# A three-layer graph kernel on TensorE: norm stages tied behind evacuations, a row addition moved to the layer before, the output stores moved off Pool, and node sums kept in PSUM

## The chip, the cores and the metric

One Trainium2 chip, one of its cores. The metric is the time of one launch on the device, in microseconds (us). Before the change it was 1362.92 us (median of 3 runs, 1360.43 to 1364.69). Besides times there is one profile of every kernel, of one of its runs; "the trace" is what that profile recorded.

Names: PE is the tensor engine, DVE the vector engine, ACT the scalar engine, Pool the GpSimd engine, SP the sync engine, which here only issues DMAs.

## The reference, cut to what matters

```python
# x: (8, 2048, 64), adj: (2048, 2048), fp32; every layer: x = x + f(relu(layernorm(x)))
# layer 0: Chebyshev terms of adj, combined with weights of each node
out = einsum('bnki,nkio->bno', [h, A h, 2 A A h - h], einsum('nd,dkio->nkio', emb, weight)) + emb @ bias
# layer 1: three steps v = W2 relu(W1 [v, A v] + b1) + b2
# layer 2: agg = A h; (agg * c) @ w_nl folded, + b_nl; then @ w_out.T + b_out
# layer 3: attention masked by adj > 0.5; elu(att @ h)
```

The kernel tests at run time that no element of adj is above 0.5 (a general path stands by). Then every row's attention is uniform, and layer 3 adds one row for each batch, elu(mean over the nodes of h). This is why the kernel needs "the sums of h": h is the normalised, rectified x after layer 2, and its sum over 2048 nodes decides one row y that is added to all of x at the end.

## The kernel before

The eight batches are worked in four pairs p; the nodes in four blocks nb of 512. The heavy work is `product`: 32 matmuls of 128x512 that multiply one block of adj with all of h, ended by one DVE instruction (the evacuation) that takes the PSUM bank to SBUF. The `fill` functions are called after some of the 16 steps of a product, to emit other work there. A tile scheduler orders each engine's queue by its own estimate; an engine runs its queue in that order.

```python
pending = []
def norm_stages(xt, name, done, out_):       # layernorm + relu, in three stages
    z = block("z", f"z_{name}", 3)           # three buffers with the tag "z"
    ...                                      # DVE mean, z = x - mean; ACT square
    yield
    ...                                      # DVE var                        (L159, L160)
    nc.gpsimd.tensor_tensor(rstd, var, mhalf, op=ALU.pow)                   # (L162)
    yield
    nc.vector.scalar_tensor_tensor(h, g, 0.0, rstd, op0=max, op1=mult)      # (L165), cut
    done(h)
    yield

def go_on():                                 # one more stage of every pending norm
    for e in list(pending):
        next(e[0]); e[1] -= 1
        if e[1] == 0: pending.remove(e)

def product(hl, nb, name, out, crow, fill={}):
    ps = bank("mm", f"bv_{name}")
    for m in range(NCH):                     # 16 steps
        ...                                  # two matmuls bv (L202)
        if m in fill: fill[m]()
    nc.vector.tensor_tensor(out, ps, crow, op=ALU.mult)      # evacuation: g or e (L208)

def keep(p, nb, acc, name):                  # end of layers 0 and 1
    nc.gpsimd.dma_start(xs[p][:, part(nb), :], acc)
    norm_relu(acc, name, lambda z: nc.gpsimd.dma_start(hs[p][:, part(nb), :], z))

def node_weights(p, nb, terms):              # layer 0
    for t in range(4):
        for dg in range(D // DG):
            ...                              # PE: y (L458); DVE: 8 x L467, accumulates into acc, odd
        go_on()
    ...

def layer2(n, p):
    zsum = lastp.tile([P, 4, 2 * C], F32, name="zsum")
    def finish(nb):
        fill_x(acc, 2, p, nb)                                        # load of x
        nc.gpsimd.tensor_tensor(acc, acc, rows4(rbo), op=ALU.add)    # row addition (L664)
        pn = back_to_nodes(e[nb], wos, f"2_{p}_{nb}")                # PE: bn (L543)
        nc.vector.tensor_tensor(acc, pn, acc, op=ALU.add)            # (L666)
        norm_relu(acc, ..., add, zsum if nb == 0 else None)          # add: zsum += h (L670)
    for nb in range(NB):
        fill = {1: go_on, 4: lambda: behind(nb), 11: go_on}          # behind: finish(nb - 1)
        e.append(product(..., fill=fill))
    finish(3)
    prepare(n + 1, 3)
    all_done()
    pS = ...                                 # PE: sum of zsum over the nodes, 4 matmuls (L692)
    ...                                      # y = elu(pS / N); acc += y (L701); 8 stores on Pool (L703)
```

## Time and profile before

| | before |
|---|---|
| time, median | 1362.92 us |
| span of the profiled run, clock | 1363.3 us, 0.967 |
| PE busy | 1266.1 us of 1363.3 |
| layer 2, first to last product | 168.6 us |
| after the last product | 26.0 us |

PE is busy for 93% of the span. The page's lines, the waits and the stretches that show it are in the prediction. Two single places more: the first product of layer 2, and the end of a pair. Timeline of the kernel before (start us, duration us, engine, line, operation, out<-in, shapes, count; in brackets how long the engine idled, and for whom):

```profile
1177.99 0.69 DVE L165 SCALAR_TENSOR_TENSOR z<-z,rstd 128x512 f32<-128x512 f32 x1 [2.14 <-POOL rstd L162]
1178.60 0.68 DVE L208 TENSOR_TENSOR e<-bv,crow 128x512 f32<-128x512 f32 x1
...
1179.33 1.16 PE L543 MATMUL bn<-wl,e 128*128 128x128 f32 x8 [2.43 <-DVE e L208]
...
1219.05 2.08 PE L692 MATMUL pS<-zsum,ones 128*128 128x128 f32 x8 [2.67 <-DVE zsum L670]
```

The first bn waits 2.43 us for e, and e waits in DVE's queue behind a norm stage of layer 1 that is waiting for Pool's rstd. At a pair's end PE idles 2.67 us until the sums of h are in zsum, and the matmuls after that run slow (2.08 us for what takes 1.05 to 1.16 elsewhere).

### The profile page before, as it was taken

To read this page: it belongs to the slowest core of one execution; us is meant where nothing else is said; L and a number is where in the kernel's file an instruction comes from. 1 tells how busy PE (TensorE), PEld (TensorE's weight loads), DVE (VectorE), ACT (ScalarE), POOL (GpSimd) and SP (SyncE) were. 2 spreads that over 40 slices of the span, in tenths; PEclk is the share of its full clock that TensorE was granted. 3 is DMA by queue.
4 is the path that set the end of the run, shared out by engine and by line. 5 is a ranking of instruction groups with operands and counts; after the bars stand their busy time and mean duration, and the time that the engine had idled before them with its cause. 6 is when DMAs were issued, how large, how long until landed. Compare 5 with 4: busy or idle time off the path is not lost. (4 is left out here: it accounts for less than half of the span.)

```text
span 1363.3 us, 16001 instructions
## 1 busy us (share of the span) xinstructions
PE 1266.1 (93%) x5904; PEld 898.6 (66%) x5904; DVE 803.7 (59%) x1949; ACT 191.2 (14%) x325; POOL 227.8 (17%) x230
## 2 busy tenths in 40 slices
PE   6899999999999999999978999999999999888883
PEld 4678555555575555755556788788788877666762
DVE  4753677767775777267778744335324424665664
ACT  4542001000010000000011111112112112111100
POOL 1310011110020001010010013004002201333443
PEclk7799999999999999999988999999999999999896
DMA  6755223212122112111067623113103212323231
GB/s 193 217 193 119 82 81 96 78 62 66 59 82 61 55 50 68 53 35 62 32 214 232 191 77 101 31 33 136 34 30 103 76 31 77 123 90 97 78 86 34
DMA packets 95595, 123.45 MB, mean 91 GB/s; under 512 B 50804, under 2 KB 52852, under 8 KB 95508
## 3 DMA queue, kind: packets, MB, share of 16 engines
q1 hardware_dynamic: 76180, 92.69, 22.5%
q0 software_dynamic: 8784, 27.41, 5.8%
q10 hardware_dynamic: 10544, 2.23, 0.8%
q8 instruction: 49, 0.80, 0.2%
q14 instruction: 38, 0.31, 0.1%
HBM read 94.90 MB, written 27.40 MB: 90 GB/s over the span
## 5 line engine op out<-in xcount | busy, mean ns | idle before, releaser
L202 PE MATMUL bv<-BT,H 128*128 128x512 f32 x1024 | 423.2, 413 | 0.0
L202 PE MATMUL bv<-BT,L 128*128 128x512 f32 x1024 | 404.6, 395 | 0.4 <-DVE L L194 0.4
L202 PEld LDWEIGHTS bv<-BT,L 128*128 128x128 f32 x1024 | 194.9, 190 | 48.5 <-issue 9.3
L202 PEld LDWEIGHTS bv<-BT,H 128*128 128x128 f32 x1024 | 194.8, 190 | 47.8 <-issue 9.3
L467 DVE SCALAR_TENSOR_TENSOR acc<-y,emb,acc 128x128 f32<-128x128 f32 x512 | 176.4, 345 | 63.4 <-PE y L458 63.2
L467 DVE SCALAR_TENSOR_TENSOR odd<-y,emb,odd 128x128 f32<-128x128 f32 x448 | 153.6, 343 | 0.0
L458 PE MATMUL y<-wt,t0T 64*128 64x512 f32 x512 | 139.9, 609 | 10.7 <-DVE odd L467 10.7
L440 POOL DMA_DIRECT2D xs<-acc x32 | 17.6, 551 | 742.1 <-DVE acc L471 382.6
L162 POOL TENSOR_TENSOR rstd<-var,mhalf 128x8 f32<-128x8 f32 x64 | 106.8, 1669 | 187.3 <-DVE var L160 179.0
L208 DVE TENSOR_TENSOR g<-bv,crow 128x512 f32<-128x512 f32 x48 | 33.1, 690 | 136.6 <-PE bv L202 136.6
L165 DVE SCALAR_TENSOR_TENSOR z<-z,rstd 128x512 f32<-128x512 f32 x60 | 51.1, 852 | 102.0 <-POOL rstd L162 102.0
L156 ACT ACTIVATE sq<-z 128x512 f32<-128x512 f32 x64 | 40.5, 633 | 454.1 <-DVE z L152 444.2
L458 PEld LDWEIGHTS y<-wt,t0T 64*128 64x128 f32 x512 | 44.1, 186 | 74.9 <-issue 69.7
L543 PE MATMUL bn<-wl,g 128*128 128x128 f32 x384 | 52.2, 280 | 8.2 <-ACT g L634 8.2
L543 PEld LDWEIGHTS bn<-wl,g 128*128 128x128 f32 x384 | 49.9, 194 | 14.1 <-ACT g L634 11.4
L580 DVE SCALAR_TENSOR_TENSOR junk<-st,cols 128x512 uint8<-128x512 f32 x64 | 48.5, 758 | 17.1 <-DMA st<-in_adj_dram 15.9
L159 DVE TENSOR_REDUCE var<-sq 128x8 f32<-128x512 f32 x64 | 43.7, 683 | 24.3 <-ACT sq L156 24.2
L215 PE MATMUL pt_adj<-ident,st 128*128 128x128 f32 x256 | 43.1, 314 | 14.1 <-DMA st<-in_adj_dram 10.4
L286 DVE TENSOR_REDUCE cols<-st 128x1 f32<-128x1024 f32 x32 | 38.9, 1216 | 27.1 <-DMA st<-in_adj_dram 27.0
L215 PEld LDWEIGHTS pt_adj<-ident,st 128*128 128x128 f32 x256 | 34.1, 161 | 24.3 <-issue 10.5
L150 DVE TENSOR_REDUCE mean<-acc 128x8 f32<-128x512 f32 x64 | 43.4, 684 | 3.9 <-DMA acc<-in_x_dram 2.3
L152 DVE TENSOR_TENSOR z<-acc,mean 128x512 f32<-128x512 f32 x64 | 43.9, 693 | 1.8 <-DVE var L160 0.3
(178 smaller groups left out, 1758.8 us busy)
## 6 DMA issues: line engine op xcount, KB each, us to landing
st<-in_adj_dram SPq DMA_DIRECT2D x32, 512.0 KB, 4.7
crow<-crowD SPq DMA_DIRECT2D x64, 256.0 KB, 3.2
st<-in_adj_dram SPq DMA_DIRECT2D x64, 256.0 KB, 3.5
hs<-z POOLq DMA_DIRECT2D x48, 256.0 KB, 3.0
hb<-hs SPq DMA_DIRECT2D x40, 256.0 KB, 3.2
xs<-acc POOLq DMA_DIRECT2D x32, 256.0 KB, 2.5
acc<-xs SPq DMA_DIRECT2D x32, 256.0 KB, 2.9
acc<-in_x_dram SPq DMA_DIRECT2D x48, 128.0 KB, 2.8
```

The costliest lines, as they stand in the source:

```text
L150: nc.vector.tensor_reduce(mean, groups(xt), axis=AX.X, op=ALU.add)
L152: nc.vector.tensor_tensor(g, groups(xt), mean[:, :, None].to_broadcast([P, 8, C]), op=ALU.subtract)
L156: nc.scalar.activation(sq, z, AF.Square)
L159: nc.vector.tensor_reduce(var, groups(sq), axis=AX.X, op=ALU.add)
L162: nc.gpsimd.tensor_tensor(rstd, var, mhalf, op=ALU.pow)
L165: nc.vector.scalar_tensor_tensor(groups(h), g, 0.0, rstd[:, :, None].to_broadcast([P, 8, C]), op0=ALU.max, op1=ALU.mult)
L202: nc.tensor.matmul(ps, hl[m // 4][i][:, m % 4, :], BT[:, nb, m, :], start=(m == 0 and i == 0), stop=(m == NCH - 1 and i == 1),)
L215: nc.tensor.transpose(pt[:, t, :], src(t), ident)
L458: nc.tensor.matmul(y[:, bb, :], terms[k][hs_, ts], wt[hs_, k, dg * 512:(dg + 1) * 512], start=(k == 0), stop=(k == K - 1),)
L467: nc.vector.scalar_tensor_tensor(xj, yd, ec, old, op0=ALU.mult, op1=ALU.add)
L543: nc.tensor.matmul(ps[:, t, :], fT[:, t * P:(t + 1) * P], wmat, start=True, stop=True)
L580: nc.vector.scalar_tensor_tensor(junk, tested[k], cols[:, i, :], tested[k], op0=ALU.not_equal, op1=ALU.logical_and, accum_out=bad[:, i, q: ...
```

## The change

Its intent: take from DVE's queue what stands ahead of an evacuation, take from Pool what slows DVE, take the additions of h from DVE, and issue the stores on queues with hardware descriptors. The core of the diff:

```diff
+    ahead = []
     def go_on():
-        for e in list(pending):
-            ...
+        with tc.issue_after(ahead.pop().ins) if ahead else nullcontext():
+            for e in list(pending):
+                ...
+        ahead.clear()
# product:
-        nc.vector.tensor_tensor(out, ps, crow, op=ALU.mult)
+        ahead.append(nc.vector.tensor_tensor(out, ps, crow, op=ALU.mult))
# node_weights: the last L467 of a tile goes into ahead before go_on
+            ahead.append(last)
             go_on()
# keep: the row of layer 2's bias is added at the end of layer 1, after the norm has read acc
-    def keep(p, nb, acc, name):
-        nc.gpsimd.dma_start(xs[p][:, part(nb), :], acc)
+    def keep(p, nb, acc, name, more=None):
         norm_relu(acc, name, lambda z: nc.gpsimd.dma_start(hs[p][:, part(nb), :], z))
+        if more is not None:
+            nc.gpsimd.tensor_tensor(acc, acc, more, op=ALU.add)
+        nc.gpsimd.dma_start(xs[p][:, part(nb), :], acc)
# layer2:
-            nc.gpsimd.tensor_tensor(acc, acc, rows4(rbo), op=ALU.add)
-            norm_relu(acc, f"3_{p}_{nb}", add, zsum if nb == 0 else None)
+            norm_relu(acc, f"3_{p}_{nb}", lambda h: z.update({nb: h}))
+        def sums(nb):
+            for t in range(4):
+                nc.tensor.matmul(pS[:, :2 * C], ones, z[nb][:, t, :],
+                    start=(nb == 0 and t == 0), stop=(nb == NB - 1 and t == 3))
         def behind(nb):
+            go_on()
-            fill = {1: go_on, 4: lambda: behind(nb), 11: go_on}
+            fill = {5: lambda: behind(nb), 12: go_on}
+            if nb > 1:
+                fill[15] = lambda: sums(nb - 2)
+        go_on()
         finish(3)
+        sums(2)
         prepare(n + 1, 3)
         all_done()
-        pS = bank("tr", f"pS_{p}")
-        for t in range(4):
-            nc.tensor.matmul(pS[:, :2 * C], ones, zsum[:, t, :], start=(t == 0), stop=(t == 3))
+        sums(3)
# the stores:
-                nc.gpsimd.dma_start(
+                (nc.scalar if p == NP - 1 and nb % 2 else nc.sync).dma_start(
```

`issue_after` orders the queue of the engine: what is emitted inside comes after the named instruction. If `ahead` is empty, nothing is ordered. The lines shift: L162 becomes L163, L165 L166, L194 L197, L202 L205, L208 L211, L458 L463, L467 L472, L543 L549, L692 L676, L703 L713; the row addition L664 becomes L445.

## The prediction

> **What bounds the kernel now.** I read the page's busy times and slices first, then the waits of TensorE, then the busy times by stretch, then single stalls in the timeline. The first three lines are from the page: busy time, then forty slices of about 34 us.
>
> ```profile
> PE 1266.1 (93%) x5904; PEld 898.6 (66%) x5904; DVE 803.7 (59%) x1949; ACT 191.2 (14%) x325; POOL 227.8 (17%) x230
> PE   6899999999999999999978999999999999888883
> PEclk7799999999999999999988999999999999999896
> ```
>
> TensorE is the bound: only 97 us of the 1363 are idle. The slices say where: the start, the change from layer 0 to layer 1 (about 690 us), and the last six, which are layer 2. Layer 1 (800 to 1168 us) is full. So Pool at 17% and DVE at 59% can matter only through waits that they give TensorE. Those are (us in total, times, longest):
>
> ```profile
> PE bn L543 <- DVE e L208: 21.5, 10, 3.1
> PE pS L692 <- DVE zsum L670: 14.2, 4, 7.4
> PE y L458 <- DVE odd L467: 10.7, 7, 2.4
> ```
>
> The first two are layer 2, the third is layer 0; all three are touched by the change. Two stretches, layer 2 up to the end of its last product, and the tail (us; PE, PEld, DVE, ACT, POOL busy with counts; granted clock; DMA share; GB/s):
>
> ```profile
> 1168.70:1337.70 169.00, 143.11 (x651) 117.23 (x650) 106.88 (x172) 17.82 (x30) 68.05 (x60) 0.94 0.29 86
> 1337.70:1363.30 25.60, 3.24 (x16) 2.75 (x16) 10.11 (x18) 0.94 (x2) 8.12 (x10) 0.57 0.18 44
> ```
>
> TensorE idles 25.9 of 169 us, at a clock of 0.94, and then the kernel runs 25.6 us without a product. One stall of layer 2 in order of time (start, duration):
>
> ```profile
> 1239.39 1.26 POOL L664 TENSOR_TENSOR acc<-acc,wl 128x512 f32<-128x512 f32 x1
> 1239.45 1.74 DVE L165 SCALAR_TENSOR_TENSOR z<-z,rstd 128x512 f32<-128x512 f32 x1 [1.83 <-POOL rstd L162]
> 1241.23 0.69 DVE L670 TENSOR_TENSOR zsum<-zsum,z 128x512 f32<-128x512 f32 x1
> 1241.84 0.68 DVE L208 TENSOR_TENSOR e<-bv,crow 128x512 f32<-128x512 f32 x1
> 1242.57 2.08 PE L543 MATMUL bn<-wl,e 128*128 128x128 f32 x8 [3.11 <-DVE e L208]
> ```
>
> The product had long ended. DVE could not evacuate it (e), because the last norm stage (L165) stood ahead of e in its queue, waited 1.83 us for Pool's rstd, ran 1.74 us instead of the 0.69 us it takes elsewhere, and was followed by the zsum addition. After 3.11 us of idleness the eight bn matmuls take 2.08 us; after shorter gaps they take 1.16. The same pattern in layer 0:
>
> ```profile
> 242.62 0.69 DVE L165 SCALAR_TENSOR_TENSOR z<-z,rstd 128x512 f32<-128x512 f32 x1 [1.85 <-POOL rstd L162]
> 243.23 0.35 DVE L467 SCALAR_TENSOR_TENSOR acc<-y,emb,acc 128x128 f32<-128x128 f32 x1
> 245.53 1.97 PE L458 MATMUL y<-wt,t0T 64*128 64x512 f32 x4 [2.10 <-DVE odd L467]
> ```
>
> **What the Trainium skill says.** (1) "SBUF — State Buffer", Who interferes with whom: a DVE instruction with two SBUF inputs contends with a GpSimd instruction that reads SBUF, and one blocks fully. The trace agrees: of the 18 L165 in layer 2, 13 start within 0.1 us after an L664 addition on Pool and take 1.74 to 1.78 us; the other five take 0.69. (2) "TensorE: Matmul & The Clock Gate", Architectural detail: ScalarE's and VectorE's queues are strict FIFO. The stall above is that. (3) Same page, What's actually happening: about 3.4 us of idleness halve the clock and about as much work restores it. Here gaps of 2.7 to 3.1 us are already followed by slices at 0.53 to 0.85, so this bites somewhat earlier, which a free-running window allows. (4) "DMA: Bandwidth & Descriptors", SWDGE vs HWDGE vs iDMA: Pool's DMAs have descriptors made by software, those of SP and ACT by hardware, with faster setup. Here one store takes 0.75 us of Pool (L703), one load 0.32 to 0.43 us of SP.
>
> **The change, part by part.** *Ties.* Every go_on now queues its DVE norm stages behind the last evacuation (or, in layer 0, behind the last L467 of a tile). In layer 2 the stages move to products' steps 5 and 12. So e runs as soon as its product ends, 0.1 + 0.68 us. bn stands 12 matmuls (12 x 0.226, start to start, = 2.7 us) into the next product: no wait. Of 21.5 us of bn waits, 2.45 belong to the last bn (tail); of the other 19.0 I keep 1 us at the first product, where stages left from layer 1 still precede e.
>
> *Row addition.* 16 Pool additions of 1.3 us move from layer 2 to the end of layer 1, where TensorE has no idle time to lose and Pool is nearly empty. L165 loses its 1.06 us extra 13 times, all off the bound once e is tied ahead; it shortens the final chain of each pair.
>
> *Sums.* The 12 zsum additions (0.69 us of DVE) go; instead TensorE does 16 blocks of 4 matmuls where it did 4. A block's 8 records cost 0.92 us, as bn does from its start to the next product's matmul (1179.33 to 1180.25). Within the stretch 14 blocks replace 3: +11 x 0.95 = +10.4 us on the bound, a real price. Blocks two products behind are ready without a wait. At the end of a pair, the chain bn, acc, mean, z, square, var, rstd, z is 7.6 us without the Pool wait, the slow L165 and the addition (10.7 before); TensorE reached the old pS 7.7 us after bn. So of 6.8 us of waits in the first three pairs about 2.5 remain.
>
> *Clock.* In layer 2 the product matmuls average 404 ns against 389 in undisturbed stretches: 505 x 15 ns = 7.6 us, with slow bn and pS about 10. With gaps below 1 us nearly all of it returns.
>
> Layer 2 up to its last product: 143.1 busy - 10 cold + 10.4 sums + 3.5 idle left + 1.5 of transitions = 148.5 us, for 169: **-20.5 us**.
>
> *Tail.* Four lines of the timeline:
>
> ```profile
> 1341.35 0.69 DVE L666 TENSOR_TENSOR acc<-bn,acc 128x512 f32<-128x512 f32 x1 [1.31 <-issue]
> 1348.64 2.08 PE L692 MATMUL pS<-zsum,ones 128*128 128x128 f32 x8 [7.39 <-DVE zsum L670]
> 1352.02 2.50 DVE L701 TENSOR_TENSOR acc<-acc,y 128x512 f32<-128x512 f32 x4
> 1353.01 6.01 POOL L703 DMA_DIRECT2D out_dram<-acc  x8 [5.87 <-DVE acc L701]
> ```
>
> e comes 1.6 us sooner, the zsum addition (0.7) is off the chain. Pool's eight stores end at 1359.0, 4.5 us after the additions; on two hardware queues the last pair is issued about 0.8 us after its addition: some 3.3 us saved with landing. Together **-5.5 us**.
>
> *Layer 0.* Four gaps of pair 0 (1.8, 1.8, 2.1, 2.4) come from L165 ahead of L467; tied, the two stages run behind the 16 L467 of the first tile. They then cost 1.4 us of DVE there, against its slack of 2 x 0.5 us (8 x 0.258 for a y that TensorE makes in 2.57), leaving about 0.4 each: 6.5 saved. Two of these gaps are followed by a clock of 0.96 over 40 us, 1.6 us each: 3 saved. A wait of 2.0 at 413 us (transposes for an evacuation behind L165) goes too. The other three y waits (2.6 us together) come from a halved operand (L194), not from a stage, and stay. With a margin for new small waits: **-10 us**.
>
> Sum: 1362.9 - 20.5 - 5.5 - 10 = 1327, which I round to **1328 us**.
>
> **Rivals.** (a) *The sums eat the gain.* The price of 10 us is on the bound; if blocks also wait for z, or break the weight-load overlap and cost 1.3 us each, layer 2 gains only 13 and the total is near 1336. For it: an unwarmed pS takes 2.08. Against: warmed, 8 records take 0.92 to 1.2. (b) *The wait moves.* Stages behind e make z late, so each pair's end, or the next pair's first e behind the y chain on DVE, stalls instead: 3 us a pair returned, near 1338. Against: 7.6 against 7.7 us, though that margin is thin. (c) *SP blocks.* The stores wait on SP for the additions, with loads of crow and acc behind them in the queue; 2 us a pair would give 1334. Against: eight issues of 0.35 us are 2.8 us, and the next loads are needed several us later. (d) *Layer 0 gives nothing*, because the stages then hold L467 elsewhere: 1338. (e) Better: the clock stays up everywhere and no gap is left, 1320.
>
> **Range and chances.** Each rival costs 6 to 10 us and two together are plausible; all of them are not. I take 1316 to 1342. The 2% line is 1335.7, some 8 us above the estimate: faster by over 2% 0.72, within 2% 0.27, slower 0.01.
>
> **What would show it.** Right: the bn wait for e below 4 us in total, L165 in layer 2 at 0.69, DVE running e before L165, pS records fourfold (128) at about 0.12 us each, clock above 0.98 in layer 2, y waits near 4 us, no store on Pool's list, and a tail of about 20 us. Wrong: bn or pS still waiting 3 us at pair ends, a clock still below 0.96, y waits of 8 us or more, or layer 1 with new idle time from the moved additions.

## The result, and the profile after

The changed kernel took **1340.24 us** (median of 4 runs, 1335.47 to 1340.92) beside 1361.68 us of the kernel before on the same chip; the ratio is 0.9836, 95% interval 0.9802 to 0.9870. A ratio is the mean time of one kernel's fast runs over that of the other's of the same rounds, so not quite the ratio of the medians quoted. It is faster by 1.6%, "the same" at a line of 2%. The prediction's range held it; its point was 12 us too low, and its likeliest class was wrong.

The page after: busy times, and the slices (tenths busy, tenths of the clock):

```profile
PE 1266.3 (95%) x6000; PEld 904.0 (68%) x6000; DVE 777.1 (58%) x1937; ACT 192.0 (14%) x325; POOL 202.9 (15%) x198
...
PE   6899999999999999999979999999999999989995
```

PE has 96 matmuls more (6000 for 5904) and the same busy time, and the span is 24 us shorter. The waits of PE after (us in total, times, longest):

```profile
PE pS L676 <- DVE z L166: 10.6, 7, 5.3
...
PE y L463 <- DVE odd L472: 8.6, 8, 2.7
...
PE bn L549 <- DVE e L211: 6.6, 3, 5.2
```

bn's wait for e fell from 21.5 to 6.6, but of that one single wait is 5.2. The wait for the sums comes seven times now, not four. The two stretches after, layer 2 to the end of its last product and the tail (columns as in the prediction):

```profile
1162.10:1317.70 155.60, 143.69 (x731) 121.12 (x730) 87.44 (x165) 17.69 (x30) 35.39 (x27) 0.98 0.33 97
1317.70:1339.10 21.40, 4.67 (x28) 3.91 (x26) 8.01 (x16) 0.94 (x2) 2.40 (x2) 0.67 0.23 54
```

PE idles 11.9 us in layer 2 for 25.9 before. To see where the 24 us came from, the span is cut at single matmuls that both kernels have: first matmuls of products, for layer 1 the first transpose of its operand, for layer 2 the matmul after layer 1's last bn, and for the tail the start of the last product matmul. A second profile of the changed kernel (e11 below), from a later chip, shows what repeats:

| stretch, us | before | after | after, again | predicted change |
|---|---|---|---|---|
| prologue | 136.7 | 138.6 | 136.2 | 0 |
| layer 0, pairs 0 and 1 | 247.3 | 238.2 | 238.5 | |
| layer 0, first terms of pair 2 | 32.8 | 30.6 | 30.6 | |
| layer 0, rest to the third part of pair 3 | 213.7 | 218.0 | 216.2 | |
| layer 0, these three | 493.8 | 486.8 | 485.3 | -10 |
| from there to layer 1 | 64.2 | 64.2 | 64.3 | 0 |
| layer 1 | 473.9 | 471.6 | 472.5 | 0 |
| layer 2, first to last product | 168.6 | 155.5 | 156.7 | -20.5 |
| tail | 26.0 | 22.3 | 21.8 | -5.5 |
| span | 1363.3 | 1339.1 | 1336.9 | -36 |

So layer 0 gave 7.0 to 8.5, layer 2 11.9 to 13.1, the tail 3.7 to 4.2. The prologue, which no run was meant to change, took 132.7 to 138.6 us over all profiles, so the span of a single profile says little, and stretches are compared instead. Three places explain what is missing. **The first product of layer 2**, after:

```profile
1166.82 1.67 DVE L197 TENSOR_TENSOR L<-hb,H 128x512 fp32r<-128x512 f32 x1
...
1169.85 1.26 POOL L445 TENSOR_TENSOR acc<-acc,wl 128x512 f32<-128x512 f32 x1 [1.07 <-DVE var L161]
1171.07 1.66 POOL L163 TENSOR_TENSOR rstd<-var,mhalf 128x8 f32<-128x8 f32 x1
1172.77 0.69 DVE L166 SCALAR_TENSOR_TENSOR z<-z,rstd 128x512 f32<-128x512 f32 x1 [2.93 <-POOL rstd L163]
...
1173.97 0.68 DVE L211 TENSOR_TENSOR e<-bv,crow 128x512 f32<-128x512 f32 x1
...
1174.71 2.07 PE L549 MATMUL bn<-wl,e 128*128 128x128 f32 x8 [5.22 <-DVE e L211]
```

The last norm of layer 1 still stands ahead of e, as before the change; its rstd now waits on Pool for a row addition (L445) that the change moved here, and the wait grew from 2.43 to 5.22 us. Two runs below bear on this growth: with the row addition back in layer 2 (e3) the first bn waits 1.19 us, and without the ties (e1) 1.34 us, so both parts of the change have a share in it. L197, with two inputs in SBUF, ran beside another such addition and took 1.67 us in place of 0.69. **The pair's end**, after:

```profile
1202.05 1.16 PE L676 MATMUL pS<-z,ones 128*128 128x128 f32 x8 [0.75 <-DVE z L166]
...
1208.52 0.69 DVE L166 SCALAR_TENSOR_TENSOR z<-z,rstd 128x512 f32<-128x512 f32 x1 [1.81 <-POOL rstd L163]
1209.27 1.16 PE L676 MATMUL pS<-z,ones 128*128 128x128 f32 x8 [1.25 <-DVE z L166]
...
1278.03 0.69 DVE L160 TENSOR_REDUCE var<-sq 128x8 f32<-128x512 f32 x1 [0.76 <-ACT sq L157]
...
1278.83 0.69 DVE L211 TENSOR_TENSOR e<-bv,crow 128x512 f32<-128x512 f32 x1
...
1279.58 1.16 PE L549 MATMUL bn<-wl,e 128*128 128x128 f32 x8 [0.54 <-DVE e L211]
```

There are two waits for h at each of three ends, for block 2 and for block 3 (0.75 and 1.25, 0.75 and 1.08, 0.74 and 0.70), and two for e (0.88, 0.54): 6.7 us in all. The last three lines show one of the waits for e: the untied variance stage of step 12 (L160) waits for ACT, and e is queued behind it. **Layer 0, pair 3**, after, a stall that was not there before:

```profile
606.94 0.69 DVE L412 COPY wz<-wP 128x512 f32<-128x512 f32 x1 [3.04 <-DMA wD<-wz]
...
608.03 1.86 PE L463 MATMUL y<-wt,t0T 64*128 64x512 f32 x4 [2.72 <-DVE odd L472]
...
610.07 0.68 DVE L166 SCALAR_TENSOR_TENSOR z<-z,rstd 128x512 f32<-128x512 f32 x1
```

DVE idles 3.04 us until a store of weights (wD) has landed, because it wants that store's buffer for wz; wz is one of the three "z" buffers, and the tied norm stage, which holds another one, now runs only at 610.07.

### The profile page after: what moved, and what is told of

It is laid out like the page before. It is cut to its first block, busy times and chain, and to the rows that moved or that the text cites. A ratio compares the mean times of both kernels' runs of the same rounds, so it can differ in the third digit from the quotient of the medians.

```text
span 1339.1 us, 16146 instructions
## 1 busy us (share of the span) xinstructions
PE 1266.3 (95%) x6000; PEld 904.0 (68%) x6000; DVE 777.1 (58%) x1937; ACT 192.0 (14%) x325; POOL 202.9 (15%) x198
## 3 DMA queue, kind: packets, MB, share of 16 engines
q1 hardware_dynamic: 90964, 96.37, 23.9%
## 4 chain that ended last, share of the span: by engine, by line
PE 75%; DVE 9%; DMA 8%; issue 3%; POOL 3%; ACT 1%; SPq 0%; ACTq 0%; POOLq 0%; DVEq 0%
PE bv L205 26%; PE y L463 22%; DMA st<-in_adj_dram 4%; PE bn L549 3%; PE ph L636 2%; PE bv_1b L205 2%; PE bv_3b L205 2%; PE bv_2b L205 2%; POOL rstd L163 2%; PE bv_2a L205 2%; PE bv_0b L205 2%; PE bv_3a L205 2%; PE bv_1a L205 2%; PE bv_0a L205 2%; PE pt_adj L218 2%
## 5 line engine op out<-in xcount | busy, mean ns | idle before, releaser
L205 PE MATMUL bv<-BT,H 128*128 128x512 f32 x1024 | 421.7, 412 | 0.0
L205 PE MATMUL bv<-BT,L 128*128 128x512 f32 x1024 | 401.4, 392 | 0.4 <-DVE L L197 0.4
L205 PEld LDWEIGHTS bv<-BT,L 128*128 128x128 f32 x1024 | 192.9, 188 | 48.2 <-issue 10.1
L205 PEld LDWEIGHTS bv<-BT,H 128*128 128x128 f32 x1024 | 192.9, 188 | 47.7 <-issue 10.1
L472 DVE SCALAR_TENSOR_TENSOR acc<-y,emb,acc 128x128 f32<-128x128 f32 x512 | 175.8, 343 | 60.5 <-PE y L463 58.8
L472 DVE SCALAR_TENSOR_TENSOR odd<-y,emb,odd 128x128 f32<-128x128 f32 x448 | 152.9, 341 | 0.0
L463 PE MATMUL y<-wt,t0T 64*128 64x512 f32 x512 | 139.9, 609 | 8.6 <-DVE odd L472 8.6
L163 POOL TENSOR_TENSOR rstd<-var,mhalf 128x8 f32<-128x8 f32 x64 | 106.4, 1665 | 235.2 <-DVE var L161 232.3
L211 DVE TENSOR_TENSOR g<-bv,crow 128x512 f32<-128x512 f32 x48 | 33.2, 691 | 156.0 <-PE bv L205 156.0
L463 PEld LDWEIGHTS y<-wt,t0T 64*128 64x128 f32 x512 | 44.3, 185 | 72.7 <-issue 65.4
L445 POOL TENSOR_TENSOR acc<-acc,wl 128x512 f32<-128x512 f32 x16 | 21.0, 1315 | 302.6 <-DVE z L153 301.3
L166 DVE SCALAR_TENSOR_TENSOR z<-z,rstd 128x512 f32<-128x512 f32 x64 | 43.6, 686 | 35.0 <-POOL rstd L163 34.8
L549 PEld LDWEIGHTS bn<-wl,g 128*128 128x128 f32 x384 | 49.3, 191 | 14.3 <-ACT g L640 10.1
L549 PE MATMUL bn<-wl,g 128*128 128x128 f32 x384 | 51.3, 276 | 6.9 <-ACT g L640 6.9
L160 DVE TENSOR_REDUCE var<-sq 128x8 f32<-128x512 f32 x64 | 43.5, 680 | 18.0 <-ACT sq L157 17.9
```

The source lines that it names most:

```text
L160: nc.vector.tensor_reduce(var, groups(sq), axis=AX.X, op=ALU.add)
L166: nc.vector.scalar_tensor_tensor(groups(h), g, 0.0, rstd[:, :, None].to_broadcast([P, 8, C]), op0=ALU.max, op1=ALU.mult)
L205: nc.tensor.matmul(ps, hl[m // 4][i][:, m % 4, :], BT[:, nb, m, :], start=(m == 0 and i == 0), stop=(m == NCH - 1 and i == 1),)
L463: nc.tensor.matmul(y[:, bb, :], terms[k][hs_, ts], wt[hs_, k, dg * 512:(dg + 1) * 512], start=(k == 0), stop=(k == K - 1),)
L472: last = nc.vector.scalar_tensor_tensor(xj, yd, ec, old, op0=ALU.mult, op1=ALU.add)
L549: nc.tensor.matmul(ps[:, t, :], fT[:, t * P:(t + 1) * P], wmat, start=True, stop=True)
```

## The experiments

All kernels gave the right result. Stretch times are cut as in the table above. The theory at the start: the three places named are where the missing gain lies (each by its own cause), and the ties, the moved addition and the PSUM sums each do what the prediction says. The rivals: ties and relief of Pool are two cures for the same wait, so one of them is idle; the sums in PSUM cost more than they give; the stores give nothing. The first eight kernels tell these apart, the last four put the answers together.

### e1: all but the ties

```diff
-        with tc.issue_after(ahead.pop().ins) if ahead else nullcontext():
+        with nullcontext():
```

> The changed kernel with the ties of DVE's norm stages taken off (nothing else; TensorE's order is nearly unchanged, DVE's is not). Theory A (the ties are the main gain, in layer 0 and in layer 2): layer 0 takes 7 us longer (its gains of 9.1 and 2.2 us go, the new wait of 2.7 us at 608 us and its slow matmuls go too), the waits of bn for e in layer 2 come back to over 10 us, total about 1358. Rival B (in layer 2 the relief of Pool and DVE alone removes the waits, since L165 no longer meets a Pool addition, no zsum addition precedes e, and bn stands two matmul pairs later): bn waits below 4 us outside the first product, total about 1347.

Measured: 1345.2 us, ratio 0.9895 (0.9866 to 0.9924). Layer 0 goes back in its first stretches (245.6 and 32.8 us, for 238.2 and 30.6), and the stall in pair 3 is gone (213.9 for 218.0). Layer 2 takes 153.1, no more than with the ties (155.5), and bn waits for e only 4.6 us in total. The line of the waits:

```profile
PE bn L549 <- DVE e L211: 4.6, 4, 2.0
```

So in layer 2 the ties add nothing on top of the rest of the change; what they are worth, they are worth in layer 0 and in the tail (24.2 us for 21.8 to 22.3, where the last bn now waits 1.97 us for e). The first product is even better off without them: its bn waits 1.34 us for 5.22. Part of this only moved, since layer 1's last bn waits 2.24 us for g in place of 0.32. But together that is 3.6 us for 5.5. In the order of the L166 stages, the ties had put one norm of layer 1 more into this product (the L166 at 1165.02; without ties its counterpart ran at 1157.89).

### e5: the ties and the new steps alone

Stages at steps 5 and 12 and the ties, as in the change; the additions into zsum, the row addition and the stores as before. In words:

```diff
-    with rows moved to keep, sums(nb) on PE, stores on SP and ACT
+    with the row addition on Pool in finish, zsum on DVE, stores on Pool
```

> The kernel before with only the ties and the stages' new steps (5 and 12); zsum on DVE, row addition on Pool in layer 2 and stores on Pool as before. e1 showed that in layer 2 the relief alone removes the waits of bn for e. Theory C (two sufficient causes: either the ties or the relief of Pool and DVE is enough): bn waits of 2 us or less outside the first product, layer 2 to its last product 148 to 154 us, total 1334 to 1341. Rival D (the relief is what is needed, ties are not enough, since a slow L166 and the zsum addition still fill DVE before e): bn waits over 8 us, total 1348 or more.

Measured: 1341.51 us, 0.9839 (0.9818 to 0.9860): the whole change's time. The waits of PE in this kernel:

```profile
PE pS L700 <- DVE zsum L676: 20.5, 4, 9.2
...
PE bn L549 <- DVE e L211: 6.8, 6, 2.4
```

bn's wait falls to 6.8 us by the ties with the new steps, although 13 of the norm stages in layer 2 still take 1.74 to 1.78 us beside the row addition on Pool. This is near theory C, but not as good: outside the first product 5.6 us of bn waits are left where it said 2 or less, and layer 2 takes 156.6 us, not 148 to 154. The wait for the sums grows from 14.2 to 20.5. With e1 this shows that bn's wait has two cures, each of which takes most of it: the ties with the new steps, or the relief with them. The change pays for both and gets one. What the new steps do alone was not run. The rest of the change shortens the waits for the sums at the three pair ends from 11.3 to 5.3 us, and the price of the sums and the first product eat that gain.

### e2: the sums of h on DVE again, the rest as changed

```diff
-            norm_relu(acc, f"3_{p}_{nb}", lambda h: z.update({nb: h}))
+            norm_relu(acc, f"3_{p}_{nb}", add, zsum if nb == 0 else None)   # zsum += h
-        sums(nb) at four places, 16 blocks of 4 matmuls
+        4 matmuls from zsum after all_done()
```

> The changed kernel with zsum added on DVE again (12 additions of 0.69 us) and one block of four matmuls per pair, in place of four blocks. Theory A (the PSUM sums are a price on the bound, 12 blocks of 0.81 to 0.92 us, which ties make needless): 8 to 11 us faster than the changed kernel in layer 2, about 1331. Rival B (the additions delay e or the end of each pair by as much as TensorE is relieved): within 3 us of the changed kernel, 1338 to 1343, with waits of bn and pS larger by 8 us or more.

Measured: 1332.1 us, 0.9796 (0.9765 to 0.9826); layer 2 150.4 us. It is faster by about 5.4 us than the whole change (0.0040 of 1361 by the ratios; layer 2 shows 5.1 to 6.3), less than the 8 to 11 that I expected. The intervals of the two ratios overlap, so the reading rests on layer 2: 150.4 us here, and 155.5, 156.7 and 157.6 in the three profiles with the change's layer 2 (the third is e7). PE waits longer for the sums at the three pair ends (2.70, 2.67, 2.08; together 7.5 for 5.3; in return the two waits for e there, 1.4 us, are gone), but ten blocks of matmuls less stand in the stretch. A block delays the next matmul by 0.80 to 0.81 us where nothing waits. The sums in PSUM are a loss in this form.

### e3: the row addition back in layer 2, on Pool

```diff
-                    keep(p, nb, acc, f"2_{p}_{nb}", rows4(rbo))
+                    keep(p, nb, acc, f"2_{p}_{nb}")
             fill_x(acc, 2, p, nb)
+            nc.gpsimd.tensor_tensor(acc, acc, rows4(rbo), op=ALU.add)
```

> The changed kernel with the row addition back on Pool in layer 2. Theory A (with e tied first, a slow L166 beside a Pool addition is off the bound): within 3 us of 1340; L166 shows durations of about 1.75 us again where it meets the addition; the first product's wait of 5.2 us is shorter, since two Pool additions no longer stand before its rstd. Rival B (the relief of Pool is what the change lives on): 1348 or more, with waits at e or at the ends of pairs.

Measured: 1340.7 us, 0.9852 (0.9822 to 0.9881): not told apart from the change. Layer 2 is 159.3 for 155.5 to 156.7, though the first bn waits only 1.19 us in place of 5.22. So moving the addition gives some 7 to 8 us to the rest of layer 2 (159.3 - 155.5 + 4.0, or 159.3 - 156.7 + 4.0) and takes about 4 back in the first product.

### e4: the stores back on Pool

```diff
-                (nc.scalar if p == NP - 1 and nb % 2 else nc.sync).dma_start(
+                nc.gpsimd.dma_start(
```

> The changed kernel with its output stores on Pool again; TensorE's order is the same. Theory A (only the last eight stores are on the path): 3 to 4 us longer, all after the last matmul, about 1343.5. Rival B (Pool's stores also delay rstd and with it the first tiles of the next pair): 6 us or more longer, with a longer distance from one pair to the next.

Measured: 1337.09 us, 0.9832 (0.9804 to 0.9860): no loss in the time. The tail alone is 23.9 us for 21.8 to 22.3, so the stores are worth some 1.6 to 2.0 us, less than the runs of a kernel differ. Why so little: the tile view of the stored tile, for the kernel before and for the one after (durations ns: least, median, most; then the time to landing):

```profile
L703 POOL DMA_DIRECT2D out_dram<-acc x32: 752/752/806, 1223.4 to 1358.3; - x32
...
DMA to landing us min/median/max: 2.5/2.8/4.4
```

```profile
L713 SPq DMA_DIRECT2D out_dram<-acc x28: 388/501/1833, 1212.4 to 1331.5; - x28
L713 ACTq DMA_DIRECT2D out_dram<-acc x4: 397/583/1243, 1330.4 to 1332.2; - x4
```

An issue on the other two queues takes 0.50 and 0.58 us at the median and up to 1.8 and 1.2, not 0.35. The last issue ends 4.4 us after the first addition of y (7.0 before), but the end of the kernel then comes 5.6 us after it, for 4.3 before: the last stores on ACT's queue take 4.9 us to land at the median, the last eight on Pool took 2.7 to 3.6. In the second profile of the change the two times are 4.9 and 4.7 us.

### e6: no norm stages of layer 1 before the first e

```diff
-            fill = {5: lambda: behind(nb), 12: go_on}
+            fill = {} if nb == 0 and n == NP else {5: lambda: behind(nb), 12: go_on}
```

(n == NP is the first pair of layer 2; the pending stages then come after its first product's evacuation.)

> The changed kernel with the norm stages left over from layer 1 run in the second product of layer 2 instead of the first, so that the first e is queued ahead of them. Theory A (the 5.2 us wait of the first bn comes from DVE's order: e behind two norms whose rstd waits on Pool behind two row additions): the wait goes, layer 2 is 5.5 to 7 us shorter, about 1334. Rival B (the pile of stages only moves on and stops the second e or the first sums): 2 us or less gained, with a new wait of 3 us or more in the second or third product.

Measured: 1332.15 us, 0.9789 (0.9765 to 0.9814); layer 2 151.1 for 155.5 to 156.7. The only wait of this kind that is left comes one product later:

```profile
1175.62 1.16 PE L549 MATMUL bn<-wl,e 128*128 128x128 f32 x8 [1.98 <-DVE e L211]
```

So the 5.2 us wait and its slow matmuls come from the untied stages, and the change could have had 4 to 6 us here.

### e7: the norm stages finished before the weights want the "z" buffers

```diff
+                ahead.clear()
+                all_done()
                 make_weights()
```

> The changed kernel with the pending norm finished, untied, before the weights are made in layer 0 (pair 3, second part). Theory A (the new wait of 2.7 us at 608 us is a z buffer that the tied stage holds longer, so that the weights' third block waits for a store to land, and DVE with it): that stretch is 213.9 us again instead of 218, about 4 us gained, total about 1336. Rival B (the wait is the weights' own DMA, which came at a bad place by chance of order): no gain, the wait stays.

Measured: 1335.28 us, 0.9795 (0.9771 to 0.9820). The stretch of layer 0 that had grown takes 214.5 for 216.2 to 218.0, and the waits show it (after: 8.6, 8, 2.7):

```profile
PE y L463 <- DVE odd L472: 5.6, 7, 1.3
```

The stall of 2.7 us is gone, so its cause, the held buffer, is shown: the stretch took 215.9 to 218.1 us in all eight profiles with the ties and without this edit, and 213.9 to 214.5 in the four with it. DVE still idles 2.82 us for a z buffer earlier (a store of h has to land), but PE loses only 0.98 us there. The total fell by more (0.0041 of 1361 is 5.6 us) than the stretch gives (1.7 to 3.5); the rest is within the intervals.

### e8: a pair's end put into the next pair's products

```diff
         for nb in range(NB):
             fill = {5: lambda: behind(nb), 12: go_on}
+            if carry and nb == 0:
+                finish3, sums2, rest = carry
+                fill = {5: lambda: (go_on(), finish3()), 9: sums2, 12: go_on}
+            elif carry and nb == 1:
+                fill[10] = rest
+                carry.clear()
-        finish(3); sums(2); ...; all_done(); sums(3)     # y, the additions and the stores follow
+        if p < NP - 1: carry.extend((lambda: finish(3), lambda: sums(2), rest))
```

> The changed kernel with a pair's end (last bn, its norm, two blocks of sums, the softmax-free row y and the stores) moved into the first and second product of the next pair. Theory A (the 6.7 us of bn and pS waits at the three pair ends come from these standing between two products): they go, layer 2 is 5 to 7 us shorter, about 1334. Rival B (the y chain and its four additions then stand before the next e on DVE): waits of bn for e of 1.5 us or more per pair take their place, gain 2 us or less.

Measured: 1331.54 us, 0.9773 (0.9753 to 0.9793), faster by over 2%; layer 2 147.2 us. Waits:

```profile
PE bn L549 <- DVE e L211: 6.2, 2, 5.2
PE pS L678 <- DVE z L166: 6.0, 2, 5.2
```

Of the waits at the ends of the first three pairs none is left (the two of pS are in the tail, the two of bn at the first product and in the tail). That is 6.7 us of waits, and layer 2 is 8.3 us shorter (9.5 beside the second profile of the change).

### e9, e10, e12, and the change once more (e11)

e9 is the change with the three repairs (e6, e7, e8). e10 is e9 with the sums of h on DVE. e12 is e10 with one thing more:

```diff
             elif carry and nb == 1:
                 fill[10] = rest            # e10: sum, y and the four additions acc += y
+            elif carry and nb == 2:        # e12: rest ends with y,
+                fill[7] = carry[2]         #      the four additions and stores come here
```

> The change with all three repairs at once (no stages between layer 1 and the first e; the norm stages drained before the node weights; a pair's end deferred into the next pair's products), PSUM sums kept. If the three stalls are separate, as I read them, the repairs add up: -7 (first product), -4 (third part of pair 3 in layer 0) and -8 (pair ends) from about 1340, less some overlap: 1321 to 1325, ratio .970 to .973. Rival, that each repair only took away a loss of the clock that another stall gives back: no better than the best single repair, 1331.

> The same three repairs, but the four tiles of h are added on VectorE (12 additions) and TensorE sums one tile a pair, as before the change. If the price of the sums in PSUM is time of TensorE alone (11 blocks of 0.8 to 0.95 us), this is 8 to 10 us faster than the kernel with the repairs and PSUM sums: 1312 to 1316, ratio about .964, layer 2 near 138 us. Rival: the additions put off e and the wait comes back, the two are alike.

> The changed kernel itself once more, on the same chip, as the ruler for the other two: ratio .9836 within .003. Its single waits should recur: about 5 us before the first bn of layer 2, 0.7 to 1.3 us twice at each pair end, about 2.7 us in the third part of pair 3 of layer 0. A wait that does not recur was chance.

Measured, on one chip: e9 1323.17 us, 0.9715 (0.9688 to 0.9741), layer 2 142.5. e10 1319.4, 0.9695 (0.9667 to 0.9723), layer 2 139.4. The change again 1339.14, 0.9839 (0.9812 to 0.9866), with the same single waits: 5.20 at the first product, 2.58 in pair 3 of layer 0, 5.2 us at the pair ends for h. So the repairs add up (16.9 us by the ratios; 14.2 us in layer 2 and 2.0 in layer 0), as the first theory of e9 had it. For e10 I was wrong by some 4 us: it beat e9 by 3.8 us only. Part of the rival was true, e's wait came back:

```profile
1238.40 2.50 DVE L727 TENSOR_TENSOR acc<-acc,y 128x512 f32<-128x512 f32 x4
...
1240.81 0.68 DVE L211 TENSOR_TENSOR e<-bv,crow 128x512 f32<-128x512 f32 x1
...
1241.55 0.38 PE L551 MATMUL bn<-wl,e 128*128 128x128 f32 x1 [1.22 <-DVE e L211]
```

Four additions of y stand ahead of e at the end of the second product, in two of the pairs (1.22 and 1.18 us), and there are three smaller waits (0.82, 0.27, 0.15). The tail, 26.0 us for 23.6 in e9, has the last addition into zsum on its chain again, and a wait for e of 1.93 (0.99 in e9).

> The kernel with the three repairs and h added on VectorE, with one thing more: a pair's four last row additions (2.5 us of VectorE), which there stood before the second product's evacuation and cost two waits of 1.2 us, are put into the third product. If the two waits are what they look like, they go and layer 2 falls from 139.4 to about 136.5 us, with about 1.7 us of bn waits for e left besides the first; the total by 2 to 3 us, 1316 to 1318, ratio .966 to .969. Rival: another evacuation is held up instead, no gain (.9695).

Measured: **1313.34 us**, 0.9639 (0.9610 to 0.9668). Layer 2 takes 134.0 us. The stretch of e12 from the first bn's wait to its last product (columns as above):

```profile
1171.00:1287.70 116.70, 115.83 (x572) 98.14 (x572) 83.81 (x155) 15.81 (x27) 22.94 (x14) 0.99 0.39 107
```

PE idles 0.9 us in 116.7. All the smaller waits went with the two large ones, so the gain (5.3 us in layer 2) was nearly twice what I expected of it. The tail is 2.1 us shorter than in e10 as well, which this edit doesn't aim at. With e9 this gives the price of the PSUM sums with nothing but the first bn (2.02 and 1.85 us) waiting for e or h on either side: 142.46 - 134.05 = 8.4 us for the ten blocks more that stand in the stretch, 0.84 us each, about what single blocks show (0.80). e12 is the fastest kernel, 3.6% under the kernel before; its sums of h are on DVE, as they were before the change.

## Why the prediction was right or wrong

**The bound and the places** were right: PE, through waits of layer 2, layer 0 and the tail, with layer 1 unmoved (-2.3 and -1.4 us in two profiles).

**Ties in layer 2: outcome right, reason half right.** bn's waits went, except the one of 5.2 us and two below 1 us. "Every go_on now queues its DVE norm stages behind the last evacuation" was not so: those at step 12 have nothing to be tied to. And e1 and e5 show two cures, each of which takes most of the wait, while the prediction counted on each part without asking what it was worth beside the others.

**The first product: the failed step, first half.** "Of the other 19.0 I keep 1 us at the first product, where stages left from layer 1 still precede e." It took 5.2. The text saw that these stages stay untied, and missed that the row additions, moved "to the end of layer 1, where TensorE has no idle time to lose and Pool is nearly empty", come just there ahead of the rstd for which DVE waits. What a stretch's average says of Pool (nearly empty) says nothing of the one moment at which Pool is on the chain. e6 shows what these stages cost, and e3 what the moved addition adds to them. The prediction did not see either that the ties themselves carry one norm more of layer 1 into this product (e1).

**The pair's end: second half.** "About 2.5 remain" of 6.8 us; 6.7 were there. The part that the text worked out, the wait for the last h, was nearly right (1.25 + 1.08 + 0.70 = 3.0 us, although the chain took 9.1 us from bn to pS, 1200.14 to 1209.27, and not 7.6: DVE ran another norm's stage and L197 before it took up bn). Two sentences about the others failed. "Blocks two products behind are ready without a wait" doesn't hold for block 2 of a pair, which is summed after product 3 with nothing in between: 0.75 + 0.75 + 0.74. And "bn stands 12 matmuls into the next product: no wait" doesn't hold for block 3, whose bn now comes after its own product with only a block of sums between: 0.88 + 0.54. In both cases e stood behind the untied stage of step 12. In the kernel before, five or six matmuls of the next pair's product had slipped in there. This is rival (b), at 2.2 us a pair for the 3 it was given. e8 shows it.

Both halves together are 8.4 us of idle time too little; layer 2 was mis-sized by 7.4 (8.6 by the second profile).

**The price of the sums** was right in kind and a little high: 0.95 us a block predicted, 0.80 measured, ten blocks more in the stretch and not eleven, so 8.0 for 10.4. The clock gave back about 7.4 of the 10 (143.11 + 8.0 - 143.69). PE's busy time of the stretch came out as predicted (143.5, measured 143.69), by two errors that cancel. Not asked in the prediction, and the main lesson of e2 and e12: whether the price buys anything. It buys shorter waits at the pair ends, and those can be had without it.

**The tail**: -3.7 to -4.2 for -5.5. The chain to the sum is shorter by what was said; the failed term is the stores, "some 3.3 us saved with landing": 1.3 to 1.8 from the first addition of y to the end (11.3 before, 10.0 and 9.5 after), 1.6 to 2.0 by e4. The duration of a load's issue on SP was taken for that of a store, and landing was taken as constant.

**Layer 0**: -7.0 to -8.5 for -10. Of the four gaps three became 0.42 each, as said; the fourth stayed at 1.73. The trace has L197 there, ahead of the first L472 and waiting 1.70 us for ACT's copy, which itself waited for a load of hb, a cause that the tie does not touch and that L165 had hidden; no run tested it. The waits of pair 2 fell (2.2 for 2.0). What the "margin for new small waits" did not hold is the single stall of 2.7 us behind a buffer (e7). "y waits near 4" was 8.6, which is one of the prediction's own signs of being wrong.

**The sum of the errors**: 3.0 (layer 0) + 7.4 (layer 2) + 1.8 (tail) - 0.4 (the rest) = 11.8 us between -36 and -24.2 (the point, 1328, lies 1 us above its own sum). The range held, since each of them was foreseen as a rival of 6 to 10 us; the chance of 0.72 for more than 2% was too high, as the rivals were added to a centre that had no share of any of them.

**What stays open**: the fourth gap of layer 0 was read and not tested, part of e7's gain is not in its stretch, the new steps were never run without the ties and the relief, and why the last stores land later on ACT's queue was not looked into.

## What to carry to other kernels

An evacuation's wait may have several causes ahead of it in the queue; before paying for several cures, see whether one suffices, and look at the first and the last turn of the loop, where the tie has nothing to tie to and moved work collides. A stage that is held back holds its buffers too: follow who takes the next one. Where the end of one unit of work has a long chain of small steps on other engines, put it under the next unit's products, before making its parts faster: here that was worth 8 us, and the sums in PSUM cost as much.

## What the Trainium skill lacked or had wrong

- "TensorE: Matmul & The Clock Gate", What's actually happening: the page gives a window of about 3.4 us of idleness, and says that it is free-running. Here shorter gaps were followed by slow matmuls or not, for no reason that these traces show: four y matmuls took 1.97 us after a gap of 2.10 and 1.13 us after one of 2.58 (in another run); eight bn or pS matmuls took 2.08 after 2.67, and 1.16 after 2.43. Over all 14 traces, no gap of 1.0 to 1.7 us before a block of bn, pS or y was followed by slow matmuls, some of those from 1.7 to 3.8 us were, and all longer ones. The page also speaks of frequent short idles between groups of matmuls, but gives no length for them.
- "DMA: Bandwidth & Descriptors", SWDGE vs HWDGE vs iDMA: "faster setup" for SP and ACT. For these stores of 128 KB an issue took 0.50 us at the median on SP and 0.58 on ACT, with up to 1.83 and 1.24, for 0.75 (never over 0.81) on Pool; those of the tail on ACT took 4.9 us to land at the median in one profile and 3.9 in the other. The gain in the tail was 1.6 to 2.0 us of 26. The page gives no duration of an issue that depends on the queue's load.
- No page that I read has the time of a power of two small operands on Pool: 1.64 to 1.66 us for 128x8, a fixed piece of every norm's chain here, and longer than DVE's 0.69 us for 128x512.
